# Second graph layer and second attention of a graph transformer: own products moved into the sums' loop, and the attention loop in a new written order

## The chip, the cores and the metric

The kernel runs on one core of a Trainium2 chip. A core has engines that run side by side, each with its own list of instructions: TensorE (PE in the profile; PEld is its loading of weights), VectorE (DVE), ScalarE (ACT), GpSimd (POOL) and SyncE (SP), which here only issues DMA transfers. They wait for each other through semaphores. The metric is the device time of one execution in microseconds (us). Before the change it is 1625.26 us, the median of three runs (1623.89 to 1626.26).

## The reference, cut to what matters

The input is x, 1250 nodes with 512 features, and a list of edges. Four parts follow each other, each added to x: a first graph layer, a dense layer with experts, a second graph layer, a second attention. The change touches the last two:

```
def L1_gnn(h):                                  # h = layernorm(x)
    own   = h @ W_self.T + bias
    neigh = (sum of h[src] over the edges into a node) / deg @ W_neigh.T
    return layernorm(own + neigh) * gamma + beta
x = x + L1_gnn(layernorm(x))

def L1_ffn(h):                                  # h = layernorm(x), 1250 x 512
    h = h + conv3(h) + pos_b                    # 3 taps along the nodes, each feature alone
    q, k, v = split(h @ qkv_w.T + qkv_b)        # 8 heads of 64
    logits  = q @ k.T * 512 ** -0.5             # 1250 x 1250 for each head
    idx     = the 16 largest of each row
    o       = softmax(logits[idx]) @ v[idx]
    return o @ wo_w.T + wo_b
x = x + L1_ffn(layernorm(x))
```

## The kernel before, in words

The nodes lie in T = 10 tiles of P = 125 rows, the 512 features in K = 4 blocks of 128. X holds the running x for all tiles. Up to about 926 us of the profiled execution the first graph layer, the first attention and the experts run; nothing of that is touched.

**Second graph layer.** The first loop (`for t in range(T)`, L1337 to L1347) normalizes a tile, transposes it on PE (four 125x125 transposes, L850), copies it to SBUF on ACT, multiplies it by w_m (W_neigh; L856) and splits the product into a high and a low half for exact sums (`split`), then multiplies the same transposed tile by w_s (W_self) and puts that product, with the bias, into `slot`. A 512-column product by a weight of 512 rows is issued as eight matmul passes. The order in this loop is left to the framework.

From L1351 on the schedule is manual: every engine runs its instructions in the written order. The sums' loop (`for t in range(T + 3)`, L1415) has per tile: `cast1` (ACT makes a column block of the edge matrix), `adj_sum1` (20 matmul passes over all tiles' halves; DVE divides by the degree, adds `slot` and takes the statistics), `scale1_` (ACT normalizes, POOL multiplies by gamma and adds to X), then two and three iterations later `stats1`/`normed1` (the next layer norm, DVE), and `turn1_` (POOL adds wo_b to X; PE transposes; ACT copies to hT; DVE copies the two edge columns that the convolution needs from the neighbour tile). `conv1` is the convolution of a range of tiles: for each k one ACT and two DVE passes. It runs for tiles 0 and 1 inside the loop and for the others behind it. `project1_` multiplies a range of tiles by w_q (DVE scales and adds the bias) and by w_k (ACT and DVE write high and low halves to K2); `values1_` multiplies by w_v. The three weights are loaded by SP into a pool of three buffers that w_m, w_s and w_q hold before.

**Second attention.** 40 steps n, one for each pair of a tile i and a pair of heads j (c = n % 4), and three more iterations to drain. The two heads of a step have three PSUM banks each for their 125x1250 scores S0 and S1; one bank serves all transposes (`ps_t`), one the outputs and the last projection (`O`). For each head a of a step:

- `halves1`: high and low halves of q for a later tile (ACT copy, POOL subtraction, two SP transfers), in steps with c < 2
- `scores1`: PE, three column chunks (512, 512, 226), two matmul passes each
- `first1`: DVE MAX8, the 8 largest of a row; POOL `nm`, their negated maximum, and `gap`
- `without1`: DVE MATCH_REPLACE8 takes those 8 out; `second1`: MAX8 again, so the 16th is known; POOL `below`, the bound
- `weights1`: ACT exp of the scores into e; `select1`: ACT sign of the scores against the bound, then POOL multiplies e by it, so what isn't selected is negative
- `turn1` and `keep1`: five groups of four PE transposes of e (both heads' ten blocks), each copied with Relu by ACT into pT; the selected weights remain
- `values1`: PE, the sum over the ten blocks for both heads; `outputs1` copies it to oT
- once a tile, `sums1` to `scale1` compute and apply the softmax's denominators; `project1` multiplies a finished tile by w_o in four parts, and `finish1` adds X (DVE y) and writes the tile out by SP.

Turns, keeps and values of step n - 1 and n - 2 are interleaved with the scores of step n and n + 1. A turn waits until the keep ahead of it has emptied the one `ps_t` bank; the scores of a head wait until the sign of that head in the step before has read the bank.

The loop's body, in the written order of before, is one line for each call in the listing below (L1672 and on). The last lines of the kernel compute a flag from the sum of signs, which tells whether every row selected 16.

Of the kernel before, what the change touches and what calls it, by code (L numbers as in the profile page):

```python
# [572 lines left out]
def tile_usual(ctx: ExitStack, tc: tile.TileContext, a: dict, out: bass.AP):  # L573
# [19 lines left out]
    def span(t0, t1):  # L593
        return slice(t0 * P, t1 * P)
# [738 lines left out]
    slot = slots.tile([128, T, D], F32, name="slot")  # L1333
    hT = slot[:, :, : K * (P + 2)].rearrange("p t (k n) -> p t k n", k=K)
    w_q = load_w(a["qkv"][:, :D], "w_q1")
    for t in range(T):
        h = work.tile([P, D], F32, name="h")  # L1337
        norm(h, X[:, t, :])
        nc.gpsimd.tensor_add(X[:, t, :], X[:, t, :], beta1)  # L1339
        xT = work.tile([128, K, P], F32, tag="xT4", name="hT1")  # L1340
        nc.scalar.copy(xT, transposed(h))
        ps = ps_mm()
        product(ps[:P], xT, 0, w_m)
        split(nb_hi[:, t, :], nb_lo[:, t, :], ps[:P])
        ps = ps_mm()
        product(ps[:P], xT, 0, w_s)
        nc.vector.tensor_add(slot[:P, t, :], ps[:P], bias1)  # L1347
    w_k = load_w(a["qkv"][:, D : 2 * D], "w_k1")
    w_v = load_w(a["qkv"][:, 2 * D :], "w_v1")

    manual = tc.manual_schedule()  # L1351
    manual.__enter__()
    xT = xc.tile([128, K, N], F32, name="xT")
    us, hs = {}, {}

    def cast1(t):
        if t < T:
            ads[t] = adj.tile([P, T, P], F32R, name="ad1")
            nc.scalar.copy(ads[t], CT[:, :, span(t, t + 1)])

    def adj_sum1(t):
        agg = ps_o()
        summed(agg[:P], ads.pop(t))
        u = work.tile([P, D], F32, name="u")
        nc.vector.scalar_tensor_tensor(u, agg[:P], deg[:, t : t + 1], slot[:P, t, :], op0=ALU.mult, op1=ALU.add)
        mv, rs = stats(work, u)
        us[t] = (u, mv, rs)

# [20 lines left out]
    def turn1_(t):  # L1389
        if not 0 <= t < T:  # L1390
            return
        nc.gpsimd.tensor_add(X[:, t, :], X[:, t, :], wo_b)
        nc.scalar.copy(hT[:, t, :, 1 : P + 1], transposed(hs.pop(t)))
        if t == 0:
            nc.vector.memset(hT[:, t, :, 0:1], 0.0)
        else:
            nc.vector.tensor_copy(hT[:, t, :, 0:1], hT[:, t - 1, :, P : P + 1])
            nc.vector.tensor_copy(hT[:, t - 1, :, P + 1 : P + 2], hT[:, t, :, 1:2])
        if t == T - 1:
            nc.vector.memset(hT[:, t, :, P + 1 : P + 2], 0.0)  # L1400

    def conv1(t0, t1):

        for k in range(K):
            c = xT[:, k, span(t0, t1)].rearrange("p (t n) -> p t n", n=P)
            at = hT[:, t0:t1, k, :]
            nc.scalar.activation(c, at[:, :, 1 : P + 1], AF.Identity, bias=pos_b[:, k : k + 1], scale=pos_m[:, k : k + 1])
            nc.vector.scalar_tensor_tensor(c, at[:, :, :P], pos_w[:, k, 0:1], c, op0=ALU.mult, op1=ALU.add)
            nc.vector.scalar_tensor_tensor(c, at[:, :, 2:], pos_w[:, k, 2:3], c, op0=ALU.mult, op1=ALU.add)

    pos_m = const.tile([128, K], F32, name="pos_m")
    nc.vector.tensor_scalar(pos_m, pos_w[:, :, 1], 1.0, None, op0=ALU.add)
    cast1(0)
    for t in range(T + 3):
        cast1(t + 1)  # L1415
        if t < T:
            adj_sum1(t)
        stats1(t - 2)
        scale1_(t)
        normed1(t - 2)  # L1420
        turn1_(t - 3)
        if t - 3 == 2:
            conv1(0, 2)
    close(work_pool, adj_pool, g1_pool, atu_pool)

# [7 lines left out]

    def project1_(t0, t1):
        n = (t1 - t0) * P
        for w in (w_q, w_k):
            for f in range(K):
                ps = ps_mm()
                for k in range(K):
                    nc.tensor.matmul(ps[:, :n], w[:, k, f * 128 : (f + 1) * 128], xT[:, k, span(t0, t1)],  # L1440
                                     start=(k == 0), stop=(k == K - 1))
                if w is w_q:
                    nc.vector.tensor_scalar(qT[:, f, span(t0, t1)], ps[:, :n], qk_b[:, f : f + 1],
                                            float(D) ** -0.5, op0=ALU.add, op1=ALU.mult)
                    continue
                for i, (own, other) in enumerate(PAIRS):
                    hi, lo = (K2[r, 2 * f + i, span(t0, t1)] for r in (own, other))
                    b = qk_b[own, K + f : K + f + 1]
                    nc.scalar.activation(hi, ps[own, :n], AF.Identity, bias=b)
                    nc.vector.scalar_tensor_tensor(lo, ps[own, :n], b, hi.bitcast(F32),  # L1450
                                                   op0=ALU.add, op1=ALU.subtract)

    def values1_(t0, t1):
        for t in range(t0, t1):
            ps = ps_mm()
            product(ps[:P], xT, t, w_v)
            nc.vector.tensor_add(V[:, t, :], ps[:P], v_b)

    conv1(2, 6)
    project1_(0, 2)  # L1460
    values1_(0, 2)
    conv1(6, 10)
    project1_(2, 6)
    values1_(2, 6)
    project1_(6, 10)
    values1_(6, 10)
# [16 lines left out]
    with (  # L1483
# [41 lines left out]
        def first1(n, a_):  # L1525
            if n > last:
                return
            i, j = steps[n]
            h = 2 * j + a_
            if h == 0:  # L1530
                bests[i] = at1.tile([P, H, TOPK], F32, name="best")
            top = bests[i][:, h, :]
            nm = at1.tile([P, 1], F32, tag=f"nm{a_}", name="nm1")
            gap = at1.tile([P, 1], F32, tag=f"gap{a_}", name="gap")
            nc.vector.max(out=top[:, 0:8], in_=score[n, a_][:, :N])  # L1535
            nc.gpsimd.tensor_scalar(nm, top[:, 0:1], -1.0, None, op0=ALU.mult)
            nc.gpsimd.tensor_scalar(gap, top[:, 7:8], -1.0, top[:, 0:1], op0=ALU.mult, op1=ALU.max)
            nc.gpsimd.tensor_scalar(gap, gap, TINY, None, op0=ALU.mult)
            found[n, a_] = (nm, gap, top)

# [9 lines left out]
        def second1(n, a_):  # L1550
# [5 lines left out]
            nc.gpsimd.tensor_scalar(below, top[:, 15:16], -1.0, gap, op0=ALU.mult, op1=ALU.add)  # L1556
            found[n, a_] = below

# [7 lines left out]
        def select1(n, a_):  # L1566
            if not 0 <= n <= last:
                return
            sg = at1.tile([P, N], F16, tag=f"sg{a_}", name="sg", bufs=1)
            nc.scalar.activation(sg, score.pop((n, a_))[:, :N], AF.Sign, bias=found.pop((n, a_)),  # L1570
                                 accum_out=signs[:, 2 * n + a_ : 2 * n + a_ + 1])
# [97 lines left out]
        with tc.manual_schedule():  # L1669
# [3 lines left out]
            for n in range(len(steps) + 3):  # L1673
# [4 lines left out]
                final = i == T - 1  # L1678
                if i is not None and i >= 0 and c == 1 and not final:
                    sums_over1(i)  # L1680
                first1(n, 0)
                values1(n - 2, 0, 5)
                select1(n - 1, 1)
                turn1(n - 1, 0)
                values1(n - 2, 5, 8)
                keep1(n - 1, 0)
                without1(n, 0)
                scores1(n, 1, 2, 1, 0)
                if n <= last and c < 2:
                    halves1(steps[n][0] + 1, c)  # L1690
                weights1(n, 0)
                turn1(n - 1, 1)
                values1(n - 2, 8, T)
                keep1(n - 1, 1)
                second1(n, 0)
                outputs1(n - 2)
                if i is not None and i >= 0:
                    if c == 0:
                        sums1(i)
                    if c == 1 and not final:  # L1700
                        sums_wide1(i)
                    if c == (1 if final else 2):
                        sums_turn1(i)
                        sums_keep1(i)
                    if c == (1 if final else 3):
                        scale1(i)
                first1(n, 1)
                select1(n, 0)
                turn1(n - 1, 2)
                if final:  # L1710
                    project1(*((i - 1, c, D // 2) if c < 2 else (i, 0, D)))
                elif i is not None and i >= 1:
                    project1(i - 1, c)
                scores1(n + 1, 0, 2)
                keep1(n - 1, 2)
                if i is not None and i >= 0 and c == 0:
                    sums_exp1(i)
                    if final:
                        sums_over1(i)
                        sums_wide1(i)  # L1720
                without1(n, 1)
                turn1(n - 1, 3)
                keep1(n - 1, 3)
                scores1(n + 1, 0, 0, 1)
                weights1(n, 1)
                turn1(n - 1, 4)
                keep1(n - 1, 4)
                second1(n, 1)
                finish1()

# [72 lines left out]
```

## Time and profile before

The profile is of one execution, which took 1624.99 us; its span is 1623.1 us, and 1.9 us lie outside.

| stage | us in the span |
|---|---|
| first loop of the second graph layer | 931.3 to 1007.0 |
| sums' loop | 1007.0 to 1079.0 |
| projections and values | 1079.0 to 1183.6 |
| attention, up to the first MAX8 of step 7 | 1183.6 to 1258.9 |
| attention, steps 7 to 38 | 1258.9 to 1578.5 |
| last step, drain, output | 1578.5 to 1623.1 |

| engine | busy us | share of the span |
|---|---|---|
| PE | 1456.4 | 90% |
| DVE | 897.3 | 55% |
| ACT | 706.6 | 44% |
| POOL | 443.1 | 27% |

A profile line names the kernel's line (L1570), the engine, the operation, the tile written and the tiles read, the shapes and a count. In a timeline the two numbers ahead of it are the start and the duration in us, and a bracket at its end gives the idle time of the engine just before and the instruction it waited for. In the list of waits the numbers are the total in us, how often, and the longest. The starts of successive instructions on one engine tell the time that each occupies; this is a little less than its duration, since neighbours overlap.

### The profile page before, as it was taken

Reading aid. Unit: us, or ns where it says so; the run is one execution under the profiler, and the core shown is the slowest. Engines: PE = TensorE matmul, PEld = TensorE weight load, DVE = VectorE, ACT = ScalarE, POOL = GpSimd, SP = SyncE. Lnnn points to the kernel's source line nnn. Section 1 sums busy time; section 2 is a strip of 40 time slices with the busy share of each in tenths; the row PEclk is TensorE's granted clock in tenths of the full one; section 3 lists DMA queues with packets and bytes.
Section 4 is the critical chain, followed back from the end, with each engine's and each line's share of the span. In section 5 each row is a group of like instructions: output and inputs, shape, how many; then the busy total and the mean of one; then the engine's idle time right before and its main releaser. Section 6 shows DMA issues by size and latency. Waiting matters only on the chain. (4 is left out here: it accounts for less than half of the span.)

```text
span 1623.1 us, 21508 instructions
## 1 busy us (share of the span) xinstructions
PE 1456.4 (90%) x8133; PEld 954.3 (59%) x8133; DVE 897.3 (55%) x1413; ACT 706.6 (44%) x1334; POOL 443.1 (27%) x634
## 2 busy tenths in 40 slices
PE   4999998868888998999999899879978999999995
PEld 2566744447777776444444445654456777777773
DVE  5985556634433332411222332764278889999992
ACT  2333433335555553111100111432157888888882
POOL 0110000011111111000000010540057888887872
PEclk8999999979999999999999999989989999999998
DMA  4001000010101010010000201000100000000000
GB/s 133 25 1 52 1 1 1 0 42 16 40 15 44 19 25 14 29 50 26 26 26 27 83 0 52 1 0 1 36 16 14 14 20 20 21 20 21 20 8 22
DMA packets 41666, 39.82 MB, mean 25 GB/s; under 512 B 25717, under 2 KB 30063, under 8 KB 41553
## 3 DMA queue, kind: packets, MB, share of 16 engines
q1 hardware_dynamic: 41553, 38.36, 8.1%
q8 instruction: 66, 1.08, 0.3%
q14 instruction: 47, 0.39, 0.1%
HBM read 25.51 MB, written 2.56 MB: 17 GB/s over the span
## 5 line engine op out<-in xcount | busy, mean ns | idle before, releaser
L1573 POOL TENSOR_TENSOR e<-e,sg 125x1250 f32<-125x1250 f32 x80 | 206.0, 2576 | 34.3 <-ACT sg L1570 33.2
L1285 DVE SCALAR_TENSOR_TENSOR X<-ps_o,gate,X 125x512 f32<-125x512 f32 x80 | 60.1, 751 | 192.5 <-PE ps_o L1283 192.5
L1521 PE MATMUL S<-K,stacks 128*125 128x512 f32 (+1 forms) x480 | 126.0, 387 | 30.7 <-ACT sg L1570 29.9
L1583 PE MATMUL ps_t<-ident,e 125*125 125x125 f32 x800 | 135.6, 293 | 12.4 <-ACT R L1624 6.0
L1283 PE MATMUL ps_o<-we,hid 128*125 128x512 f32 x320 | 141.0, 595 | 0.0
L1590 ACT ACTIVATE pT<-ps_t 125x500 f32<-125x500 f32 x200 | 117.9, 589 | 47.8 <-PE ps_t L1583 46.9
L1583 PEld LDWEIGHTS ps_t<-ident,e 125*125 125x125 f32 x800 | 108.6, 191 | 48.0 <-ACT pT L1590 27.5
L1535 DVE MAX8 best<-S 125x8 f32<-125x1250 f32 x80 | 116.9, 1462 | 34.8 <-PE S L1521 33.5
L1275 PE MATMUL ps_mm<-yT,we 128*128 128x500 f32 (+1 forms) x352 | 127.6, 521 | 0.3 <-DVE gate L1183 0.3
L1278 ACT ACTIVATE hid<-ps_mm,b 128x500 f32<-128x500 f32 (+1 forms) x44 | 26.9, 611 | 220.6 <-PE ps_mm L1275 220.6
L1555 DVE MAX8 best<-rest 125x8 f32<-125x1250 f32 x80 | 117.1, 1464 | 2.8
L1546 DVE MATCH_REPLACE8 rest<-best,S 125x1250 f32<-125x1250 f32 x80 | 116.0, 1450 | 0.0
L1060 PE MATMUL S<-K,stacks 128*125 128x512 f32 (+10 forms) x288 | 87.1, 413 | 29.9 <-ACT e L1082 25.3
L1570 ACT ACTIVATE sg<-S,below 125x1250 f16<-125x1250 f32 x80 | 104.8, 1310 | 18.0 <-POOL below L1556 18.0
L1639 PE MATMUL O<-pT,V 125*64 125x125 f32 x1600 | 112.6, 279 | 0.0
L1521 PEld LDWEIGHTS S<-K,stacks 128*125 128x125 f32 x480 | 76.3, 193 | 52.1 <-ACT sg L1570 36.2
L1563 ACT ACTIVATE e<-S,nm 125x1250 f32<-125x1250 f32 x80 | 104.1, 1302 | 2.3 <-DVE rest L1546 1.1
L1108 ACT COPY pT<-ps_t 125x500 f32<-125x500 f32 (+3 forms) x112 | 54.9, 490 | 113.9 <-PE ps_t L1103 113.4
L1339 POOL TENSOR_TENSOR X<-X,beta 125x512 f32<-125x512 f32 x10 | 13.4, 1359 | 329.0 <-DVE h L639 328.3
L1275 PEld LDWEIGHTS ps_mm<-yT,we 128*128 128x128 f32 x352 | 66.9, 191 | 61.0 <-issue 58.6
L1283 PEld LDWEIGHTS ps_o<-we,hid 128*125 128x125 f32 x320 | 59.2, 187 | 71.6 <-issue 71.3
L990 POOL TENSOR_TENSOR stacks<-yT,stacks 64x125 fp32r<-64x125 f32 x80 | 34.1, 426 | 230.0 <-ACT stacks L989 226.6
(225 smaller groups left out, 2669.7 us busy)
## 6 DMA issues: line engine op xcount, KB each, us to landing
we<-in_W SPq DMA_DIRECT2D x16, 512.0 KB
stacks<-stacks SPq DMA_DIRECT2D x160, 31.2 KB
stacks<-stacks SPq DMA_DIRECT2D x40, 125.0 KB
X<-in_x SPq DMA_DIRECT2D x5, 500.0 KB
out<-y SPq DMA_DIRECT2D x10, 250.0 KB
w_n<-in_wn SPq DMA_DIRECT2D x1, 1024.0 KB
w_c<-in_wc SPq DMA_DIRECT2D x1, 1024.0 KB
w_q<-in_Wq SPq DMA_DIRECT2D x1, 1024.0 KB
```

What stands on the lines that cost most here:

```text
L1275: nc.tensor.matmul(ps[:, :n], w1[:, k, f * 128 : (f + 1) * 128], yT[:, k, span(t0, t1)], start=(k == 0), stop=(k == K - 1))
L1283: nc.tensor.matmul(ps[:P], hid[:, f, span(t, t + 1)], w2[:, f, :], start=(f == 0), stop=(f == FF // 128 - 1))
L1521: nc.tensor.matmul(score[n, a_][:, n0:n1], stacks[i][:, x, h, :], K2[:, h, n0:n1], start=(x == 0), stop=(x == 1))
L1535: nc.vector.max(out=top[:, 0:8], in_=score[n, a_][:, :N])
L1546: nc.vector.match_replace(out=rest, in_to_replace=top[:, 0:8], in_values=score[n, a_][:, :N], imm_value=LOWEST)
L1555: nc.vector.max(out=top[:, 8:16], in_=rest)
L1563: nc.scalar.activation(e, score[n, a_][:, :N], AF.Exp, bias=found[n, a_][0])
L1570: nc.scalar.activation(sg, score.pop((n, a_))[:, :N], AF.Sign, bias=found.pop((n, a_)), accum_out=signs[:, 2 * n + a_ : 2 * n + a_ + 1])
L1573: nc.gpsimd.tensor_mul(e, e, sg)
L1583: nc.tensor.transpose(turned[n, g][:P, span(b - g0, b - g0 + 1)], es[n, b // T][:, span(b % T, b % T + 1)], ident[:P, :P])
L1590: nc.scalar.activation(pTs[n][:, g0:g1, :], turned.pop((n, g))[:P, : (g1 - g0) * P].rearrange("p (t n) -> p t n", n=P), AF.Relu)
L1639: nc.tensor.matmul(outs[n][a_ * DH : (a_ + 1) * DH, :P], V[:, t, h * DH : (h + 1) * DH], pT[:, a_ * T + t, :], start=(t == 0), stop=(t == ...
```

## The change

In the graph layer the first loop keeps the w_m product alone; the transposed tile is copied into `slot` (as `inT`), and the w_s product is made in the sums' loop, one tile in each iteration, by the new `own1`. `joined1` holds what `adj_sum1` did behind its matmuls. The loop has T iterations instead of T + 3, with shorter distances between its parts. The convolution of tiles 0 and 1 is spread over iterations 4 to 7, that of tiles 2 to 5 starts in iterations 8 and 9. The edge columns are copied by ACT instead of DVE, and wo_b is added to X during the last projections. w_v is loaded ahead of w_k.

In the attention loop the functions are the same, apart from `gap`, which leaves `first1` and becomes `gap1`. Their order is new for every engine.

```diff
+    inT = slot[:, :, : K * P].rearrange("p t (k n) -> p t k n", k=K)
...
-        nc.scalar.copy(xT, transposed(h))
+        nc.scalar.copy(inT[:, t, :, :], transposed(h))
...
-        ps = ps_mm()
-        product(ps[:P], xT, 0, w_s)
-        nc.vector.tensor_add(slot[:P, t, :], ps[:P], bias1)
...
+    for w, c in ((w_v, 2), (w_k, 1)):
+        nc.sync.dma_start(w, a["qkv"][:, c * D : (c + 1) * D].rearrange("(k p) f -> p k f", p=128))
...
+    def own1(t):
+        ps = ps_mm()
+        product(ps[:P], inT[:, t, :, :], 0, w_s)
+        us[t] = work.tile([P, D], F32, name="u")
+        nc.vector.tensor_add(us[t], ps[:P], bias1)
...
+    def joined1(t):
+        u = us[t]
+        nc.vector.scalar_tensor_tensor(u, aggs.pop(t)[:P], deg[:, t : t + 1], u, op0=ALU.mult, op1=ALU.add)
+        us[t] = (u, *stats(work, u))
...
-        nc.gpsimd.tensor_add(X[:, t, :], X[:, t, :], wo_b)
...
-            nc.vector.tensor_copy(hT[:, t, :, 0:1], hT[:, t - 1, :, P : P + 1])
-            nc.vector.tensor_copy(hT[:, t - 1, :, P + 1 : P + 2], hT[:, t, :, 1:2])
+            nc.scalar.copy(hT[:, t, :, 0:1], hT[:, t - 1, :, P : P + 1])
+            nc.scalar.copy(hT[:, t - 1, :, P + 1 : P + 2], hT[:, t, :, 1:2])
...
+    for t in range(T):
+        cast1(t + 1)
+        own1(t)
+        turn1_(t - 2)
+        adj_sum1(t)
+        if 4 <= t < 8:
+            conv1(0, 2, t - 4)
+        elif t >= 8:
+            conv1(2, 6, *((0, 1) if t == 8 else (2,)))
+        stats1(t - 1)
+        normed1(t - 1)
+        joined1(t)
+        scale1_(t)
...
+    turn1_(T - 2)
+    project1_(0, 2, w_q, 0, 1)
+    conv1(2, 6, 3)
+    project1_(0, 2, w_q, 2, 3)
+    stats1(T - 1)
+    normed1(T - 1)
+    project1_(0, 2, w_k, 0)
+    turn1_(T - 1)
+    close(work_pool)
+    project1_(0, 2, w_k, 1, 2, 3)
     values1_(0, 2)
+    for f in range(K):
+        project1_(2, 6, w_q, f)
+        conv1(6, 10, f)
+    for f in range(K):
+        project1_(2, 6, w_k, f)
     values1_(2, 6)
+    for w in (w_q, w_k):
+        for f in range(K):
+            project1_(6, 10, w, f)
+            nc.gpsimd.tensor_add(X[:, f + 4 * (w is w_k), :], X[:, f + 4 * (w is w_k), :], wo_b)
...
     values1_(6, 10)
```

The attention loop's body after the change, whole:

```
                end = i is not None and i >= 0
                values1(n - 2, 0, 5)
                values1(n - 2, 5, 8)
                if end and c == 0:
                    sums1(i)
                first1(n, 0)
                without1(n, 0)
                turn1(n - 1, 0)
                values1(n - 2, 8, T)
                gap1(n, 0)
                select1(n - 1, 1)
                second1(n, 0)
                keep1(n - 1, 0)
                scores1(n, 1, 1)
                if n <= last and c < 2:
                    halves1(steps[n][0] + 1, c)
                outputs1(n - 2)
                if end and c == 0:
                    sums_exp1(i)
                    if final:
                        sums_over1(i)
                        sums_wide1(i)
                turn1(n - 1, 1)
                keep1(n - 1, 1)
                if end and c == (1 if final else 3):
                    if final:
                        sums_turn1(i)
                        sums_keep1(i)
                    scale1(i)
                scores1(n, 1, 2)
                weights1(n, 0)
                scores1(n, 1, 0)
                if end and c == 2 and not final:
                    sums_turn1(i)
                    sums_keep1(i)
                first1(n, 1)
                gap1(n, 1)
                if final:
                    project1(*((i - 1, c, D // 2) if c < 2 else (i, 0, D)))
                elif i is not None and i >= 1:
                    project1(i - 1, c)
                finish1()
                without1(n, 1)
                turn1(n - 1, 2)
                select1(n, 0)
                if end and c == 1 and not final:
                    sums_over1(i)
                keep1(n - 1, 2)
                turn1(n - 1, 3)
                second1(n, 1)
                scores1(n + 1, 0, 0, 2, 1)
                weights1(n, 1)
                keep1(n - 1, 3)
                turn1(n - 1, 4)
                if end and c == 1 and not final:
                    sums_wide1(i)
                keep1(n - 1, 4)
```

## The prediction

> **What bounds the kernel now.** I first cut the span into stages with the table of windows. Its columns are length, busy time of PE, PEld, DVE, ACT and POOL (with counts), granted PE clock, DMA share, GB/s.
>
> ```profile
> core 0: us, PE busy (x) PEld busy (x) DVE busy (x) ACT busy (x) POOL busy (x), PEclk, DMA share, GB/s
> 931.30:1007.00 75.70, 75.51 (x199) 34.60 (x197) 22.04 (x51) 12.08 (x27) 11.68 (x9) 0.98 0.02 6
> 1007.00:1079.00 72.00, 54.70 (x238) 42.05 (x237) 50.17 (x136) 26.65 (x51) 38.03 (x30) 0.92 0.07 23
> 1079.00:1183.60 104.60, 103.21 (x274) 51.97 (x272) 40.67 (x64) 21.94 (x35) 2.89 (x3) 0.99 0.05 15
> 1258.90:1578.50 319.60, 294.26 (x2587) 237.65 (x2586) 291.19 (x304) 267.63 (x415) 257.07 (x359) 1.00 0.08 18
> ```
>
> The first loop of the graph layer (row 1) and the projections (row 3) are PE-bound. The sums' loop (row 2) is not: PE idles 17.3 us there at clock 0.92. The PE timeline shows where: its last transposes wait for DVE.
>
> ```profile
> 1070.61 0.65 PE L850 MATMUL ps_tp<-ident,h 125*128 125x125 f32 x4 [4.45 <-DVE h L639]
> 1074.92 1.09 PE L850 MATMUL ps_tp<-ident,h 125*128 125x125 f32 x4 [3.67 <-DVE h L639]
> 1078.22 1.10 PE L850 MATMUL ps_tp<-ident,h 125*128 125x125 f32 x4 [2.20 <-DVE h L639]
> ```
>
> In the attention loop (row 4) DVE is busy 91% and PE 92%. Its waits:
>
> ```profile
> DVE best L1535 <- PE S L1521: 23.8, 24, 1.4
> ...
> PE S L1521 <- ACT sg L1570: 16.5, 15, 1.3
> ACT sg L1570 <- POOL below L1556: 14.9, 14, 1.3
> ```
>
> Read upwards this is one chain: the small `below` on POOL is late, so `sign` on ACT, so the scores that overwrite its bank, so the next MAX8. The timeline of one step (POOL, ACT, then PE) shows why:
>
> ```profile
> 1321.15 2.58 POOL L1573 TENSOR_TENSOR e<-e,sg 125x1250 f32<-125x1250 f32 x1 [0.37 <-ACT sg L1570]
> 1323.81 1.07 POOL L1507 TENSOR_TENSOR stacks<-qT,stacks 64x500 fp32r<-64x500 f32 x1
> 1324.98 0.27 POOL L1556 TENSOR_SCALAR below<-best,gap 125x1 f32<-125x1 f32 x1
> ...
> 1325.28 1.30 ACT L1570 ACTIVATE sg<-S,below 125x1250 f16<-125x1250 f32 x1 [1.08 <-POOL below L1556]
> ...
> 1326.72 0.48 PE L1521 MATMUL S<-K,stacks 128*125 128x226 f32 x2 [1.11 <-ACT sg L1570]
> ```
>
> A multiply and a subtraction stand ahead of `below`. From the first MAX8 of step 7 (1258.87) to that of step 39 (1578.47) a step takes 319.6/32 = 9.99 us. The floor by DVE's own instructions is 2 x (1.51 max + 0.08 load + 1.45 match_replace + 1.38 second max) + 0.19 y = 9.03, with 0.5 more in every fourth step: 9.15 in the mean.
>
> **Graph layer, first loop.** Two tiles take 75.7/5 = 15.14 us. Two w_s products leave, 3.435 us each by the starts of successive products; 8.13 us remain (two products 6.87, eight transposes 0.78, 0.48 of waiting for the copy, which the w_s product used to cover). Five pairs: the loop ends at about 972.5, 35 us sooner.
>
> **Sums' loop.** Now each tile issues its w_s product (3.44), 20 sum passes (4.63) and, in eight iterations, four transposes (0.37): 10 x 8.07 + 8 x 0.37 = 83.7, end at 1056. DVE's chain per tile (join 0.74, two sets of statistics about 1.3 each, h 0.6, own add 0.7, and inside it ACT's 0.8 and POOL's 1.28 and 1.30) is about 8.3 us, barely under PE's 8.4, so cover is thin: the convolution pieces (two 0.5 us DVE passes for two tiles, about twice that for four) put DVE 2.5 us late at the end. I take waits of 2.5 and 0.7 us for the last two turns; bounds 0 and 8. The edge copies on ACT (DVE's took 0.85 and 0.16) hide in ACT's idle time: 26.65 us busy of 72.
>
> **Projections.** 104.6, less 1.4 idle and 0.9 of cold clock (nine first matmuls took 3.25 us), plus 0.8 for the turns moved into them: 103.1. End 1056.2 + 3.2 + 103.1 = 1162.5 against 1183.6: **-21 us** (-18 to -24.5). The ten wo_b adds leave a POOL queue with 38 us of work in the sums' loop for one with 2.9: nothing, since X's next reader is far off. On SP's queue w_v goes ahead of w_k, which waits until the last w_s product frees its buffer (about 1050); a 1 MB weight landed in about 5 us, and w_k's first product starts after four q groups, about 1064. Without that slack it would cost PE the rest of those 5 us.
>
> **Attention loop.** POOL's subtraction now stands behind `below`, and `gap` ahead of the multiply, so the old chain goes. What takes its place I found by following what each instruction waits for. exp(n,1) now stands ahead of `keep` 3 on ACT, and waits for match_replace(n,1). Behind it are queued keep 3 and keep 4; for keep 3 waits turn 4 (one PSUM bank is shared by the turns); behind turn 4 on PE stand the values and scores(n+1,1), for which MAX8(n+1,1) waits. A closed circle, once per step, start to start:
>
> - turn 1: 0.45; scores of 226 and 512 columns: 0.91; handover 0.04
> - MAX8, y, match_replace: 3.10; handover 0.09; exp 1.18; keep 3: 0.59; handover 0.05
> - turn 4: 0.54; values, 32 passes: 1.87; turn 0: 0.63; values, 8 passes: 0.58; scores of 512: 0.52
>
> Sum **10.55 us** for every step, against 9.99. The circle without it (sign, keep 2, turn 3, scores, MAX8) gives 10.04, POOL's 9. The 32 steady steps: 32 x 0.56 = +17.9. The first seven (73.0 us before) come out 0.4 shorter. The last sign stands 12.0 us behind the last step's start instead of 10.4: +1.6. What follows it (34.2 us from that sign to the end, with a POOL reduction and idle stretches of POOL of 5.55 and 7.22 us in it) is unchanged. Sum **+19 us**, bounds +10 (a handover or occupancy 0.3 us smaller) and +28. The project and y steps lie in the circle's slack on PE but y's 0.19 is in it. halves' two SP transfers and y's output transfer move within a step; stacks are needed two steps later (20 us), so nothing, and 1 us a tile if that cover were gone.
>
> **Sum.** 1624.99 (the profiled run: span 1623.1 and 1.9 around it) - 21 + 19 = **1623**. The median of the runs is 1625.26, 0.3 above that run.
>
> [...] The new loop leaves PE idle about 1.4 us between turns 2 and 3 and 0.5 ahead of turn 4 (2.5 together in steps without projection). The windows of before:
>
> ```profile
> 1225.00:1235.00 10.00, 8.11 (x73) 6.34 (x73) 9.58 (x11) 8.45 (x15) 8.23 (x13) 1.00 0.13 26
> 1235.00:1245.00 10.00, 8.67 (x67) 6.93 (x65) 7.60 (x9) 8.48 (x13) 7.62 (x13) 0.83 0.12 25
> ...
> 1275.00:1425.00 150.00, 136.88 (x1206) 110.52 (x1204) 135.24 (x142) 125.14 (x194) 119.80 (x167) 1.00 0.08 19
> ```
>
> The clock fell to 0.83 around 1240, where PE never idled over 1.8 us, yet held 1.00 over 150 us of steps with 1.1 us gaps. [...] By the row, one drop costs about 0.17 x 10 = 1.7 us on a circle half of which is PE. [...]
>
> **Rivals.**
> - *The loop gains (0.17).* The circle is not closed as I read it, or its pieces overlap; then DVE's floor decides, with 0.2 of losses 9.35 us a step: 32 x -0.64 = -20, in all about 1583 (1575 to 1605). For it: the wait of DVE's 23.8 us vanishes, nothing else names a limit. Against: exp, keep 3 and turn 4 are tied in written order, and every duration is measured.
> - *PE is throttled in the new loop (0.22), slower.* Place: between turns 2 and 4. Price 1.7 us a step hit; it decides from 4 of the 40 steps on (5.5/1.7). With ten steps 1640, with twenty 1657 (1629 to 1660). For it: 1235 to 1255. Against: 1275 to 1425.
> - *DVE bounds the sums' loop (0.10), slower.* Each tile takes 9.7 instead of 8.4: +12, about 1635 (1629 to 1642). For it: the three waits for h above. Against: the own add and the copies leave DVE and its row has 22 us free.
>
> **How the numbers follow.** The case summed above has 0.51 and its own range 1612 to 1633. A measurement here tells 0.2%, 3.25 us, from no change: 1622.0 to 1628.5. Of the 0.51, 0.22 lie below, 0.14 inside, 0.15 above. Faster 0.17 + 0.22 = 0.39; same 0.14; slower 0.22 + 0.10 + 0.15 = 0.47. The range 1601 to 1645 leaves out some 0.10 of the first rival and 0.09 of the second.
>
> **What would show it.** First loop about 41 us, sums' loop 84 with PE idle under 4, attention starting at 1163. In the loop: steps of 10.55 alike over the four c; DVE's MAX8 of the second head waiting some 1.4 us for scores each step; `sign` no longer waiting for `below` at length; keep 3 directly behind exp. Wrong if steps are near 9.3 (first rival), if clock is under 0.95 in 1200 to 1560 (second), or if the transposes in the sums' loop still wait for h (third).

## The result

The changed kernel takes 1640.67 us, the median of four runs (1639.53 to 1644.19). The kernel before, run beside it, takes 1624.58 us. The ratio is 1.0101, with a 95% interval of 1.0083 to 1.0119: it is 1% slower. The forecast was 1623 us, no change, in its likeliest case (a chance of 0.51, and a range of its own from 1612 to 1633), and slower had a chance of 0.47 over all cases. The measured time lies inside the whole range of 1601 to 1645, but 7.7 us above that case's own: the sum came out too low. The profiled execution took 1641.28 us, its span is 1639.5 us, 16.4 us more than that of before.

The table of windows of the changed kernel, with the same columns as in the prediction, follows. The second row ends at 1056.00, near where the forecast put the end of the sums' loop; its last products end at 1057.5. The last line is the kernel before, over its first seven attention steps:

```profile
core 0: us, PE busy (x) PEld busy (x) DVE busy (x) ACT busy (x) POOL busy (x), PEclk, DMA share, GB/s
930.39:972.17 41.78, 40.59 (x114) 19.15 (x114) 16.74 (x41) 11.07 (x26) 11.03 (x9) 0.96 0.00 1
972.17:1056.00 83.83, 83.10 (x308) 54.04 (x307) 46.25 (x118) 29.40 (x61) 21.10 (x17) 1.00 0.07 26
1056.00:1075.44 19.44, 13.68 (x55) 11.27 (x54) 13.09 (x25) 4.25 (x13) 12.55 (x10) 0.82 0.00 0
1075.44:1169.50 94.06, 93.23 (x235) 43.61 (x233) 33.64 (x51) 19.59 (x33) 7.80 (x7) 1.00 0.06 17
1169.50:1248.40 78.90, 58.68 (x412) 46.65 (x413) 62.50 (x58) 54.97 (x80) 51.76 (x74) 0.85 0.06 14
1248.40:1593.30 344.90, 289.37 (x2585) 237.50 (x2584) 291.28 (x304) 270.58 (x414) 257.61 (x359) 0.99 0.07 17
...
1184.30:1258.87 74.57, 59.04 (x412) 46.22 (x413) 62.55 (x60) 54.53 (x80) 51.58 (x74) 0.86 0.07 15
```

The reader is to see four things. The sums' loop is now full of matmuls (83.1 of 83.8 us, clock 1.00). Behind it stand 19.4 us in which PE is busy for only 13.7, at a mean clock of 0.82. Over the first steps of the attention the mean clock is 0.85, hardly another than before (0.86), although these steps now take longer. And the steady stage, which took 319.6 us before, takes 344.9 with every engine about as busy as it was.

Set side by side by the first MAX8 of steps 0, 7 and 39, the 16.4 us are:

| part | before | after | difference | forecast |
|---|---|---|---|---|
| first w_m product to first w_v product | 164.1 | 150.1 | -14.0 | -21 |
| what lies ahead of it in the span (untouched) | 931.35 | 930.39 | -1.0 | 0 |
| step 0 to step 7 | 73.0 | 77.5 | +4.5 | -0.4 |
| step 7 to step 39 | 319.6 | 344.9 | +25.3 | +17.9 |
| from step 39's first MAX8 to the end | 44.6 | 46.2 | +1.6 | +1.6 |

The projections behind the first w_v product are the same in both (90.4 us from it to the first MAX8 of step 0).

The waits in the steady stage (us in total, how often, the longest):

```profile
PE ps_t L1613 <- ACT pT L1620: 53.6, 48, 2.3
DVE best L1558 <- PE S L1545: 49.7, 59, 2.3
...
ACT e L1593 <- DVE rest L1576: 7.0, 24, 0.3
```

The chain below, sign, scores is gone from the list. In its place PE waits 53.6 us for the copies that empty the bank of the turns, where before it waited 0.8 us for them, and DVE waits 49.7 us for scores instead of 23.8. One step of the timeline shows the circle itself, DVE first, then ACT, then PE:

```profile
1438.78 1.47 DVE L1558 MAX8 best<-S 125x8 f32<-125x1250 f32 x1 [1.22 <-PE S L1545]
1440.17 0.27 DVE L1694 TENSOR_TENSOR y<-X,O 125x128 f32<-125x128 f32 x1
...
1440.43 1.45 DVE L1576 MATCH_REPLACE8 rest<-best,S 125x1250 f32<-125x1250 f32 x1
...
1441.97 1.31 ACT L1593 ACTIVATE e<-S,nm 125x1250 f32<-125x1250 f32 x1 [0.33 <-DVE rest L1576]
1443.17 0.58 ACT L1620 ACTIVATE pT<-ps_t 125x500 f32<-125x500 f32 x1
...
1443.80 0.70 PE L1613 MATMUL ps_t<-ident,e 125*125 125x125 f32 x4 [0.26 <-ACT pT L1620]
1444.43 1.83 PE L1669 MATMUL O<-pT,V 125*64 125x125 f32 x30
```

MAX8, y, match_replace, exp, keep 3, turn 4 and values follow each other with gaps under 0.1 us, as the circle was drawn. A step is called throttled here when a drop of the PE clock falls into it. Where none does, the lengths are 10.42, 10.54, 10.75 and 10.95 us in turn, by the first head's MAX8. Measured along the circle itself (from turn 1 to the next turn 1, steps 21 to 35) it is 10.61 us, and 10.82 in the step with c = 2. The forecast was 10.55.

### The profile page after: what moved, and what is told of

The parts are those of the page before. It is cut to its first block, busy times and chain, and to the rows that moved or that the text cites. A ratio compares the mean times of both kernels' runs of the same rounds, so it can differ in the third digit from the quotient of the medians.

```text
span 1639.5 us, 21481 instructions
## 1 busy us (share of the span) xinstructions
PE 1450.1 (88%) x8133; PEld 956.8 (58%) x8133; DVE 892.0 (54%) x1395; ACT 712.5 (43%) x1352; POOL 445.0 (27%) x634
## 5 line engine op out<-in xcount | busy, mean ns | idle before, releaser
L1613 PE MATMUL ps_t<-ident,e 125*125 125x125 f32 x800 | 138.9, 298 | 73.0 <-ACT pT L1620 70.6
L1593 ACT ACTIVATE e<-S,nm 125x1250 f32<-125x1250 f32 x80 | 104.2, 1303 | 10.3 <-DVE rest L1576 9.4
L1669 PE MATMUL O<-pT,V 125*64 125x125 f32 x1600 | 108.5, 284 | 0.0
L1669 PEld LDWEIGHTS O<-pT,V 125*64 125x64 f32 x1600 | 89.6, 142 | 10.0 <-issue 1.5
```

The lines of the kernel that those rows point to most:

```text
L1593: nc.scalar.activation(e, score[n, a_][:, :N], AF.Exp, bias=found[n, a_][0])
L1613: nc.tensor.transpose(turned[n, g][:P, span(b - g0, b - g0 + 1)], es[n, b // T][:, span(b % T, b % T + 1)], ident[:P, :P])
L1669: nc.tensor.matmul(outs[n][a_ * DH : (a_ + 1) * DH, :P], V[:, t, h * DH : (h + 1) * DH], pT[:, a_ * T + t, :], start=(t == 0), stop=(t == ...
```

## The experiments

The theory after the result: the two parts add up, the loop is held by the circle, and the clock takes a further share in some steps; the missing gain of the graph layer lies in the last two tiles. Rivals: the loop is slow through the clock alone; the parts disturb each other.

**The graph layer alone.** The diff's first part, with the old attention loop.

> The graph layer of the change with the attention loop of before. If the two parts add up: the values end some 14 us earlier, the loop keeps its 9.99 us a step (first MAX8 of step 7 to that of step 39), and the whole is 1610, 0.991 of before. If the new graph layer harms the attention loop (another phase of the clock, q and K2 later): over 1616.

Measured: 1610.92 us, ratio 0.9903 (0.9876 to 0.9930). From first w_m to first w_v product 150.2 us, and 319.4 us from step 7 to 39, so 9.98 us a step. The parts do not disturb each other in this direction.

**The attention loop alone.** The old graph layer with the new loop.

> The graph layer of before with the attention loop of the change. If the parts add up: attention starts at 1184 as before and the whole is 1624.6 + 31 = 1655, steps 10.4 to 10.95 without throttle. If the late start of the loop is what throttles it: 1645 or less.

Measured: 1658.54 us, ratio 1.0195 (1.0169 to 1.0221). The two ratios, 0.9903 and 1.0195, add up to 1.0% over the time before, which is what both together gave. Unthrottled steps are again 10.41 to 10.96 us, but more of them are throttled here: steps ending at 3, 4, 7, 8 and 11 took 13.64, 12.95, 13.44, 13.04 and 12.15 us.

**One pair of lines swapped.**

```diff
-                weights1(n, 1)
                 keep1(n - 1, 3)
+                weights1(n, 1)
                 turn1(n - 1, 4)
```

> The changed kernel with one pair of lines swapped: keep 3 of the step before stands ahead of exp(n,1) on ACT, instead of behind it. Theory of the circle (exp, keep 3, turn 4, values, scores, MAX8): the circle opens, the next one (sign, keep 2, turn 3, scores, MAX8) gives 10.04, in the step with the denominators' turn 0.4 more, about 10.15 in the mean of unthrottled steps: 32 x -0.5 = -16 and some throttled steps fewer, about 1620 to 1625. Rival, the loop is slow through the PE clock alone: 1639 to 1643, as the gaps stay. Rival, another order on DVE or POOL binds: steps of 10.55 as before, 1640.

Measured: 1616.98 us, ratio 0.9939 (0.9917 to 0.9960), which is 1.6% below the changed kernel by the two ratios. The traced execution was the slowest of the five (1624.47 us). Its steps are 10.02, 10.22, 10.57 and 10.16 us; the mean from step 7 to 39 is 10.24, where 10.15 was expected. In the ACT timeline keep 3 is now done before the exp starts, so turn 4 no longer waits for it:

```profile
1444.46 0.59 ACT L1620 ACTIVATE pT<-ps_t 125x500 f32<-125x500 f32 x1 [0.79 <-PE ps_t L1613]
1444.95 1.30 ACT L1593 ACTIVATE e<-S,nm 125x1250 f32<-125x1250 f32 x1
```

DVE's wait for scores falls from 49.7 to 32.2 us:

```profile
DVE best L1558 <- PE S L1545: 32.2, 57, 0.8
```

This shows that the circle through exp and keep 3 set the pace. The loop from step 7 to 39 is still 8 us longer than the old one. That the next circle, through sign and keep 2, now sets the pace fits its forecast of 10.04 us, but no edit here tests it.

**PE work in the gap.** Four matmuls into the output bank, which nobody reads, ahead of turn 3.

```diff
+        def warm1(n):
+            if 1 <= n <= last:
+                idle = ps_o1.tile([128, 512], F32, tag="o", name="O")
+                for x in range(4):
+                    nc.tensor.matmul(idle, K2[:, x, :128], K2[:, x, :512], start=True, stop=True)
...
                 keep1(n - 1, 2)
+                warm1(n)
                 turn1(n - 1, 3)
```

> The changed kernel with four matmuls of 512 columns added between turn 2 and turn 3 of every step, into the output bank, which nobody reads: 4 x 0.25 = 1.0 us of PE work inside a gap of 1.4 to 2.25 us. Theory that gaps of PE throttle its clock in steps 3 to 5 (11.65, 12.39, 12.95 us) and in some later ones: these fall to 10.5 to 10.9, clock 1.00 in the loop, 1631 to 1633. Theory of the circle: steps that are unthrottled stay at 10.42 to 10.95. If gaps are not what throttles: 1640 to 1642, the slow steps stay.

Measured: 1633.9 us, ratio 1.0049 (1.0032 to 1.0067). So work that is thrown away makes the kernel about 0.5% faster. One of the steps 3 to 5 in the changed kernel, by its gap and what follows it on PE:

```profile
1210.82 1.20 PE L1613 MATMUL ps_t<-ident,e 125*125 125x125 f32 x4 [2.25 <-ACT pT L1620]
1211.68 2.47 PE L1545 MATMUL S<-K,stacks 128*125 128x512 f32 x6
```

The same place with the added work:

```profile
1209.56 1.18 PE L1704 MATMUL O<-K 128*128 128x512 f32 x4
1212.05 0.70 PE L1613 MATMUL ps_t<-ident,e 125*125 125x125 f32 x4 [1.31 <-ACT pT L1620]
1212.51 1.40 PE L1545 MATMUL S<-K,stacks 128*125 128x512 f32 x6
```

Six score matmuls take 2.47 us behind a gap of 2.25, and 1.40 behind one of 1.31. The steps that end at 3, 4 and 5 fall from 11.65, 12.39 and 12.95 us to 10.91, 10.55 and 10.55. From step 7 on, none is longer than 10.97 but the last, which takes 11.1 in both kernels. The unthrottled steps have not moved, so the circle and the clock are two separate causes. The windows of the changed kernel for its steps 3 to 5 and for a long undisturbed stretch:

```profile
1201.00:1227.00 26.00, 21.50 (x147) 17.70 (x147) 17.84 (x16) 16.84 (x27) 15.95 (x24) 0.76 0.05 10
...
1381.00:1550.00 169.00, 141.29 (x1288) 116.32 (x1284) 144.53 (x152) 135.02 (x208) 128.85 (x179) 1.00 0.08 19
```

Short windows show which step is hit. In the traces here a drop halves the clock (0.50) for 3.41 us or a multiple of it, and the drops of one trace start whole multiples of 3.41 us apart: in the attention loop of the changed kernel, behind its first step, at 1200.0, 1210.3, 1223.9, 1258.0, 1322.9 and 1367.3. Cut on that grid, two steps with the same longest gap of 1.77 us look like this:

```profile
1363.88:1367.29 3.41, 1.64 (x12) 1.32 (x10) 3.38 (x7) 3.22 (x6) 2.76 (x5) 1.00 0.18 38
1367.29:1370.70 3.41, 3.41 (x24) 2.73 (x24) 3.08 (x4) 2.12 (x4) 2.10 (x6) 0.50 0.02 5
...
1408.25:1411.66 3.41, 1.85 (x10) 1.32 (x10) 3.31 (x6) 3.22 (x5) 3.01 (x4) 1.00 0.18 40
1411.66:1415.07 3.41, 3.31 (x44) 2.91 (x46) 3.33 (x4) 2.00 (x5) 2.36 (x7) 1.00 0.00 0
```

The first gap lies inside one window, and PE is busy for 48% of that; the second starts just ahead of a window's edge, and PE is busy for 54% of what follows. So it is PE's busy share of such a window that goes with a drop, more than the length of one gap. From step 0 to step 39 of the 14 kernels traced here, all 26 windows at full clock with PE busy under 46% were followed by a drop (14 of them are the wait at the loop's start), 15 of 89 from 46 to 56%, and 5 of 1429 above; in the two traces of before and after alone it is 6 of 6, 4 of 18 and 1 of 199. Behind that wait, the added matmuls leave no window under 57%, and the clock stays at 1.00:

```profile
1190.00:1587.00 397.00, 368.50 (x3107) 290.89 (x3106) 338.62 (x347) 314.61 (x481) 298.46 (x415) 1.00 0.07 16
```

In a kernel with the same loop, the one without wo_b below, other steps are hit (those that end at 5, 7, 8 and 11 take 12.93, 11.43, 12.61 and 11.88 us).

**The same with transposes.** Eight transposes of X in place of the four matmuls.

```diff
-                for x in range(4):
-                    nc.tensor.matmul(idle, K2[:, x, :128], K2[:, x, :512], start=True, stop=True)
+                for x in range(8):
+                    nc.tensor.transpose(idle[:, span(x % 4, x % 4 + 1)], X[:, 0, :128], ident[:P, :P])
```

> As the kernel with four matmuls added between turn 2 and turn 3 of every step, but with eight transposes of 128 columns instead, again about 1.0 us of PE work whose result nobody reads. If transposes count for the clock as matmuls do: steps 3 to 5 at 10.5 to 10.9 and the whole at 1633. If they don't: some of these steps stay at 11.6 to 13 us, clock under 0.95 before step 7, 1638 to 1643.

Measured: 1634.08 us, ratio 1.0067 (1.0040 to 1.0094); by the whole time alone this is not told apart from the changed kernel (1.0083 to 1.0119). The trace tells more: steps 3 to 5 take 10.91, 10.57 and 10.54 us, from step 7 to the last but one none is longer than 10.97, and the clock never drops from 1190 us to step 39:

```profile
1190.00:1588.00 398.00, 365.14 (x3260) 297.94 (x3258) 339.52 (x349) 315.86 (x483) 299.65 (x417) 1.00 0.07 16
```

No window behind the loop's start has PE busy under 58%, with the transposes counted. In this trace, then, the transposes hold the clock as the matmuls do.

**The convolution out of the last iterations.** The changed graph layer loses time at the two last turns:

```profile
1061.62 1.09 PE L850 MATMUL ps_tp<-ident,h 125*128 125x125 f32 x4 [4.08 <-DVE h L639]
1062.51 9.09 PE L1422 MATMUL ps_mm<-xT,w_q 128*128 128x250 f32 x32
1071.43 1.85 PE L1422 MATMUL ps_mm<-xT,w_k 128*128 128x250 f32 x8
1074.96 0.65 PE L850 MATMUL ps_tp<-ident,h 125*128 125x125 f32 x4 [1.68 <-DVE h L639]
```

Edited in the kernel with the new graph layer and the old loop:

```diff
         if 4 <= t < 8:
             conv1(0, 2, t - 4)
-        elif t >= 8:
-            conv1(2, 6, *((0, 1) if t == 8 else (2,)))
...
     project1_(0, 2, w_q, 0, 1)
-    conv1(2, 6, 3)
+    conv1(2, 6, 0)
     project1_(0, 2, w_q, 2, 3)
...
-    project1_(0, 2, w_k, 1, 2, 3)
+    for k in range(1, K):
+        conv1(2, 6, k)
+        project1_(0, 2, w_k, k)
```

> The new graph layer with the attention loop of before, and the convolution of tiles 2 to 5 taken out of iterations 8 and 9 of the sums' loop and put beside the first projections. Theory that these pieces hold DVE (a wait of 3.0 us for ACT's convolution pass, and 2.9 us of DVE) and so make h of tiles 8 and 9 late: the waits for h (4.1, 1.7 and 0.7 us in the changed kernel) go, and with them the slow clock behind; -6 against 1611, 1604 to 1606. Rival, DVE's own chain without the convolution is as late: 1609 to 1611. Rival, the convolution then delays project1_(2, 6): 1611 or more.

Measured: 1610.75 us, ratio 0.9886 (0.9843 to 0.9929). Against the graph layer alone (0.9903) the whole can't be told apart, the intervals overlap. The stage can: from first w_m to first w_v product it takes 147.2 us instead of 150.2. The wait ahead of tile 8 falls from 4.08 to 1.11 us, and the 32 w_q matmuls behind it take 6.92 instead of 9.09. But the wait of tile 9 rises:

```profile
1063.81 0.65 PE L850 MATMUL ps_tp<-ident,h 125*128 125x125 f32 x4 [1.11 <-DVE h L639]
1064.29 6.92 PE L1422 MATMUL ps_mm<-xT,w_q 128*128 128x250 f32 x32
...
1075.88 0.65 PE L850 MATMUL ps_tp<-ident,h 125*128 125x125 f32 x4 [2.99 <-DVE h L639]
```

So half of the expected 6 us came. The pieces did make tile 8 late; moved, the first of them stands on DVE ahead of tile 9's statistics. POOL has X of tile 9 ready at 1069.78, and DVE, with the two passes of that piece (1.70 and 1.63 us from 1068.61 on) and two of q behind them, begins them at 1072.66. The slow clock moved too: behind tile 9's turn the 24 w_k products take 6.92 us here and 5.23 in the changed kernel.

**Without wo_b.** The ten additions of wo_b are left out of the changed kernel, so the bias of the last projection is missing in the output.

> The changed kernel without the ten additions of wo_b to X, so the bias of the last projection is left out of the output. In the changed kernel eight of them run on POOL from 1067.5 to 1078.5, and the DVE passes beside them took 1.62 (convolution, else 0.74) and 1.32 us (h, else 0.55). Theory that POOL's additions slow DVE's passes on SBUF: these fall to 0.74 and 0.55, the turn of tile 9 starts some 1.5 us sooner after that of tile 8 (13.3 us in the changed kernel), and the rest stays. Rival, these durations have another cause: they stay over 1.3.

Measured: 1640.07 us, in a single run. DVE in the changed kernel, where eight additions run on POOL from 1067.54 to 1078.48:

```profile
1068.65 0.73 DVE L1412 SCALAR_TENSOR_TENSOR xT<-slot,pos_w,xT 128x500 f32<-128x500 f32 x1
1069.42 1.62 DVE L1413 SCALAR_TENSOR_TENSOR xT<-slot,pos_w,xT 128x500 f32<-128x500 f32 x1
1070.97 0.47 DVE L1425 TENSOR_SCALAR qT<-ps_mm,qk_b 128x250 f32<-128x250 f32 x1
...
1073.58 1.32 DVE L639 TENSOR_SCALAR h<-X,mv,rs 125x512 f32<-125x512 f32 x1 [0.27 <-ACT rs L635]
```

And without them:

```profile
1070.68 0.73 DVE L1412 SCALAR_TENSOR_TENSOR xT<-slot,pos_w,xT 128x500 f32<-128x500 f32 x1
1071.44 0.74 DVE L1413 SCALAR_TENSOR_TENSOR xT<-slot,pos_w,xT 128x500 f32<-128x500 f32 x1
...
1075.61 0.55 DVE L639 TENSOR_SCALAR h<-X,mv,rs 125x512 f32<-125x512 f32 x1 [0.27 <-ACT rs L635]
```

The two passes fall from 1.62 to 0.74 and from 1.32 to 0.55 us, while the pass that reads PSUM (qT, 0.47) was not stretched. From the turn of tile 8 to that of tile 9 it is 12.55 us instead of 13.34: 0.8 us gained, where 1.5 were expected, since DVE now waits 1.09 us for PE's last w_q products, whose scaling stands ahead of tile 9's statistics in its written order. In the listing the additions come only during the last projections, but POOL reached them at 1067.54, with nothing ahead of them to wait for. Not every pass beside them is stretched: the one just ahead of the first of the two took 0.73 us in both kernels.

**The old loop's wait.** With the new graph layer and the old loop, `halves1` is called behind `second1(n, 0)`, so that POOL's subtraction stands behind `below`.

```diff
-                if n <= last and c < 2:
-                    halves1(steps[n][0] + 1, c)
                 weights1(n, 0)
...
                 second1(n, 0)
+                if n <= last and c < 2:
+                    halves1(steps[n][0] + 1, c)
                 outputs1(n - 2)
```

> The new graph layer with the attention loop of before, in which halves1 is called behind second1(n,0), so that POOL's subtraction no longer stands ahead of below. Theory that this stood behind the waits of the old loop (below, sign, scores, MAX8): the steps with c = 0 and 1 (10.07 and 10.43 us) fall to about 9.3 and 9.6, in all 10 x 1.6 = -16 against 1611, 1595. Rival, the multiply ahead of below is enough to hold it: the steps stay, 1611. Rival, the later ACT copy of halves delays sign instead: 1611 to 1620.

Measured: 1607.12 us, ratio 0.9873 (0.9833 to 0.9913), by the intervals not told apart from the graph layer alone. The steps tell more: the one with c = 0 falls from between 10.1 and 10.3 to 9.53 us, where 9.3 was expected. The one with c = 1 falls only from between 10.4 and 10.6 to between 10.0 and 10.2, where 9.6 was expected, and the one with c = 2 even rises from 10.25 to between 10.4 and 10.6. Four steps take 39.3 us instead of 39.9, some 40% of what was expected. ACT's wait for `below` falls from 14.7 to 5.4 us; what is left may lie in the copies of `halves` and R on ACT, ahead of sign, which a kernel below moves.

**The denominators' turn moved.** In the last kernel, moved from the middle of the step: `sums_turn1` and `sums_keep1` at the end of the step with c = 2.

```diff
-                    if c == (1 if final else 2):
+                    if c == 1 and final:
                         sums_turn1(i)
                         sums_keep1(i)
...
                 keep1(n - 1, 4)
+                if i is not None and i >= 0 and c == 2 and not final:
+                    sums_turn1(i)
+                    sums_keep1(i)
                 second1(n, 1)
```

> As the kernel before it in this list, and the transposes of the denominators with their copy moved from the middle of the step with c = 2 to its end. Theory that they delay turn 2 and what follows on PE through the one bank for turns: the step with c = 2 falls from 10.25 to about 9.4, -8 more, 1587. Rival, that step is slow for another reason: no change from 1595.

Measured: 1612.08 us, ratio 0.9896 (0.9860 to 0.9932). The step with c = 2 falls to 9.6 to 9.8 us, and the next one rises from 9.28 to 10.9: the wait has moved, with 0.8 us added.

**The three edits together.** The edits of the last two kernels and the late convolution.

> The three edits of this list together. If they add up: 1611 - 16 - 8 - 6 = 1581, 0.973 of before. If the loop without its waits is held by DVE alone, a step takes 9.15 to 9.3.

Measured: 1608.97 us, ratio 0.9886 (0.9845 to 0.9927), where 0.973 was expected. The graph stage is 146.8 us, the steps are as in the kernel just before.

**Spread further.** From the kernel with the late convolution: `halves1` in steps with c = 0 and 3, the denominators' turn behind exp(n,1) and ahead of turn 4.

```diff
                 second1(n, 0)
+                if n <= last and c in (0, 3):
+                    halves1(steps[n][0] + 1, min(c, 1))
...
                 weights1(n, 1)
+                if i is not None and i >= 0 and c == 2 and not final:
+                    sums_turn1(i)
+                    sums_keep1(i)
                 turn1(n - 1, 4)
```

> The new graph layer with the convolution of tiles 2 to 5 beside the first projections; the attention loop of before with halves1 behind second1(n,0) in the steps with c = 0 and 3 instead of 0 and 1, and the denominators' transposes and copy behind exp(n,1) in the step with c = 2. Theory that the ACT copies of halves and of R ahead of sign are what still holds the steps with c = 1 and 2: these fall from 10.1 and 10.5 to 9.6 and 9.8, and c = 3 rises from 9.28 to 9.5: 38.4 us for four steps instead of 39.4, so the whole is 0.981 of before. Rival, turn 4 waits for R and the copies only move: 39.5 or more for four steps, 0.985 to 0.99.

Measured: 1615.09 us, ratio 0.9938 (0.9921 to 0.9956). The steps with c = 1 and 2 are 9.5 to 9.7 and 9.2, so the two copies did hold them, but c = 3 takes 11.7 and c = 0 10.3 to 10.5. In the PE timeline turn 4 waits for the copy R:

```profile
1321.71 0.59 PE L1644 MATMUL ps_t<-ident,rb 125*128 125x125 f32 x4
1323.27 0.70 PE L1607 MATMUL ps_t<-ident,e 125*125 125x125 f32 x4 [0.96 <-ACT R L1648]
```

That is the mechanism of the changed kernel again: a sixth use of the one bank, behind exp on ACT and ahead of turn 4 on PE.

**The best of both.** The new graph layer with the late convolution, the old loop with `halves1` behind `second1(n, 0)` and nothing else.

> The new graph layer with the convolution of tiles 2 to 5 beside the first projections, and the attention loop of before with halves1 behind second1(n,0) in the steps with c = 0 and 1. If the two single gains add up (graph stage 3 us shorter than in the changed kernel, four steps 39.4 us instead of 40.0): 0.985 of before, about 1601 where before takes 1625. If the second gain is taken back as in the kernels that moved more: 0.988 or more.

Measured: 1601.22 us (1600.21 to 1604.63), ratio 0.9851 (0.9826 to 0.9876), as expected. It beats both kernels: 25 us below the one before and, by the two ratios, 2.5% below the changed one. It is not told apart by the intervals from the kernels with one of its two edits (0.9886 and 0.9873).

## Why the prediction was wrong

**What held.** The first loop took 41.8 us, where 972.5 us as its end meant 41.2. (The working behind it has a slip: 15.14 less 6.87 is 8.27 us for a pair of tiles, not 8.13.) The sums' loop, up to the end of its last products, took 85.4 against 83.7, with one wait of 0.7 in it. The end came out at +1.6 as forecast. The circle in the attention loop was found before the run, with the right members: 10.55 forecast, 10.61 measured, 10.82 in the step with c = 2; the swapped pair of lines confirms it. POOL's chain went as forecast. The forecast that graph layer and loop pull in opposite directions is shown by the two kernels with one part each.

**What failed.** The sum of -21 and +19 was small, so each term's size decided the sign. The clock was put at nothing and two terms were mis-sized, all the same way:

- *The clock in the attention loop, put at nothing: the +19 has no term for it.* No run shows that this loop's gaps cost nothing; in its place the runs showed some 8.4 us: with PE work in the gap, steps 0 to 7 take 72.8 us instead of 77.5, and steps 7 to 39 341.1 instead of 344.9. The two ratios give the same, 0.52%. The price per step was put at 1.7 us and reached 2.4 (12.95 against 10.55). Nor were the gaps those of the row with 1.00: PE idled up to 1.29 us there (not 1.1), and in the new loop 1.63 to 1.78 in most steady steps and 2.25 in the steps without projection, where 1.4 was foreseen. No gap between 1190 and 1590 was longer than 2.39. The other row of before (clock 0.83, gaps up to 1.8 us) was the better witness: ahead of its drop at 1235.1 PE was busy for 1.62 of 3.41 us. The text itself wrote that the first steps would have 2.5 us of idle time together, and still gave the first seven steps a gain of 0.4 us; there the row should have been charged. The sign that it named, a clock under 0.95 from 1200 to 1560, was too coarse to show the loss: it was 0.97 there.
- *The step "waits of 2.5 and 0.7 us for the last two turns; bounds 0 and 8".* They were 4.08 and 1.68, with 0.73 more one tile earlier: 3.3 us over. Behind the first of them the clock halved for 6.8 us, which cost 2.6 us more (the 32 w_q products and the turn ahead of them, against the same in the kernel with the late convolution), and the step had no term for it. The upper bound of the waits held; the value taken was too low, and the -14 lies outside the -18 to -24.5 that was worked out from it. What made DVE late was not only its own convolution passes: it waited 3.0 us for ACT's, which stood behind the cast and the copy of the turn in ACT's written order. And the ten wo_b adds, put at nothing by POOL's queue alone, cost 0.8 us there, by the one trace without them.
- *"The 32 steady steps: 32 x 0.56."* Without throttle the mean step is 10.66, because in c = 2 the denominators' transposes stand on PE ahead of the product that y waits for, so that match_replace starts 0.2 us later there, and the circle elsewhere is 10.61, not 10.55: 3.6 us.

By the table, forecast and profiled run differ by 7.0 us in the graph layer, 4.9 in the first seven steps and 7.4 in the steady ones, less 1.0 ahead of the change: 18.3 us, and the forecast was 2 us below the kernel before, the run 16.4 above. Of the 7.0, the waits, the slow clock and the first loop (0.6) explain 6.5; of the 4.9, the clock 4.7; of the 7.4, the clock 3.8 and the circle 3.6.

The second rival thus came true in part, together with the forecast's own mechanism, and the third one in the last tiles only. These two were written as alternatives to the main case, each on top of nothing; they were in truth additions to it, with the same sign.

**What stays open.** Which windows with PE busy between 46 and 56% bring a drop is not settled (one with 1.63 of 3.41 us at 1449.2 brought none), nor why five of about 61% brought one. No run varies the busy share alone, so that it is this share that drops the clock is read from the traces and from the two kernels with added work. Step lengths are those of one traced execution for each kernel.

## What to carry to other kernels

When engines run in written order, look for the closed circle, not for the longest wait: removing one wait is worth only the distance to the next circle (here from 10.66 us a step to 10.24), and a copy that empties a shared PSUM bank must not stand behind a long instruction that waits for another engine (the swap of two lines was worth 1.6%). Sum the members of each circle from occupancies and compare it with the floor of the busiest engine; in the tries here that moved a piece of work (the convolution, `halves`, the denominators' turn twice), a part of its price, or more than all of it, moved with it. When PE has gaps in every step, look at its busy share in short stretches (of 3.41 us here), and not at the longest gap alone. Where a forecast is the small difference of two large terms, charge every known loss in the sum instead of listing it as a rival.

## What the runs showed of the hardware that was not expected

- The PE clock fell to 0.50 for multiples of 3.41 us behind windows of that length in which PE was busy for 34 to 50%, with no single gap over 2.39 us (changed kernel, 1190 to 1590).
- PE work whose result nobody reads made the kernel 0.5% faster (1.0049 against 1.0101): the clock stayed at 1.00 from 1190 us to step 39, where the changed kernel's mean is 0.97; eight f32 transposes kept the steps as short as four matmuls did (10.91, 10.57 and 10.54 us against 10.91, 10.55 and 10.55).
- A DVE pass that works on SBUF took 1.62 us instead of 0.74, and another 1.32 instead of 0.55, beside POOL's additions of 1.3 us each; without these they were at 0.74 and 0.55. The pass just ahead of the first of them took 0.73 us in both kernels, and the pass behind it, which reads PSUM, 0.47; what sets the stretched ones apart no run here shows.
